# Decoder, layer 3 cross attention: 128 (head, token) rows a unit instead of 100

## The chip, the cores and the metric

One Trainium2 chip, one of its cores. The metric is the device time of one execution in microseconds (us), the median of several runs. The profile is one further execution, taken by the hardware profiler. Engines are written as the profile writes them: PE is TensorE (PEld its weight loads), DVE is VectorE, ACT is ScalarE, POOL is GpSimd, SP is the engine whose queue issues most DMAs.

## The reference, cut to what matters

The program is a four-layer decoder for 16 images of 100 text tokens, width 128, float32. Each layer has self attention, cross attention to 1444 context vectors of width 96 per image, and a feed-forward block. Only the attention part of layer 3's cross attention is changed:

```
Q = (x_text @ Wq).reshape(Bb, Tt, H, DH)          # 16 images, 100 tokens, 4 heads of 32
K = (x_vision @ Wk).reshape(Bb, Gg, H, DH)        # 1444 keys an image
scores = jnp.einsum('bthd,bghd->bhtg', Q, K) / np.sqrt(DH)
scores = jnp.where(vision_mask[:, None, None, :], scores, -jnp.inf)
topv, topi = jax.lax.top_k(scores, K_TOP)         # K_TOP = 32
probs = jax.nn.softmax(topv, axis=-1)
attn = jnp.zeros_like(scores).at[bi, hi, ti, topi].set(probs)
attn_mean = attn.mean(axis=1)                     # over the 4 heads
c_t = jnp.einsum('btg,bgd->btd', attn_mean, x_vision @ Wv)
c_t = c_t * text_mask[..., None]
```

So every one of 16 x 4 x 100 = 6400 score rows of 1444 numbers has its 32 largest found, the softmax is taken over these alone, the four heads are averaged, and the average weighs the context. `c_t` (tile `CT` in the kernel) then steers the rest of the layer: a norm, a long convolution over tokens (`kern`), and a feed-forward block.

## The kernel before, in words

The kernel is written with a tile framework: the author writes tiles and operations, a scheduler orders the instructions of each engine, and semaphores are put in where a tile is written and read, or its buffer is used again. An engine executes its own list strictly in order. A pool with `bufs=n` hands out n buffers in turn; who asks for one more waits until the oldest has been read for the last time.

The whole program runs layer after layer. The changed stage, `l3_xattn`, begins with small weight products (`xattn_weights`), the layer norm of `X` into `XN` (DVE and POOL, L264) and its transpose into `XT` (`turn`). Then it loops over the images `b`:

- `fetch(b)` brings in the context twice: `ct` (channels in partitions, for the scores; its last row is filled by POOL at L1330 from the byte mask `vm`) and `cn` (keys in partitions, for the weighted sum). Both come through SP's queue, one image ahead.
- `queries` folds the key projection into the query: 4 small matmuls on PE (L635), then one DVE add (L637). The result `qk` has 4 heads x 100 tokens as columns.
- `head(b, h, qk)` treats one head: 100 rows. Three matmuls (L1340) put 100 x 1444 scores into one of two PSUM score buffers (`psS`, `bufs=2`, three banks each). DVE then finds the 32 largest of every row in four rounds of `max` (the 8 largest of a row, L1346) and `match_replace` (overwrites those 8 by a mark, L1347), the first round from PSUM and the others in the copy `wk`. ACT computes the exponential of all scores (L1352, bias `nm`, the negated row maximum). One more DVE pass (L1354) keeps the exponential where the mark stands, sets the rest to zero and adds up the row. Small DVE operations give `rs`, one over the sum times 0.25 times the token's mask; ACT multiplies the row by `rs` (L1361, L1363), and POOL adds the heads into `AM` (L1364).
- `mean(b - 1)`, emitted in the middle of image b: 12 transposes of `AM` (L1371), three ACT copies (L1374), 12 matmuls with `cn` (L1377), a copy `cc`, one matmul with the value weights (L1382) and the copy into `CT` (L1383).

Two score buffers and three `cn` buffers let PE run ahead of DVE. After the stage come the norm, the convolution (99 DVE passes, L1431) and the feed-forward blocks.

Of the kernel before, what the change touches and what calls it, by code (L numbers as in the profile page):

```python
# [9 lines left out]
F32 = mybir.dt.float32  # L10
U8 = mybir.dt.uint8
AF = mybir.ActivationFunctionType
ALU = mybir.AluOpType
AX = mybir.AxisListType
PSUM = bass.MemoryType.PSUM

B, S, D = 16, 100, 128
NT = B * S
G4 = 4 * S
NG = B // 4  # L20
CK = 1444
CD = 96
CA = CD + 1
NCH = 12
CKP = NCH * 128
NH = 16
BIG = 1e30
MARK = -3e38
# [13 lines left out]
def _layout(i):  # L42
    f = np.float32
    arr = {}
# [3 lines left out]
    ctx = i["ctx_768"]  # L48
    arr["ctxT"] = np.concatenate([ctx.transpose(0, 2, 1), np.ones((B, 1, CK), f)], axis=1)
    cn = np.zeros((B, CKP, CA), f)  # L50
# [2 lines left out]
    arr["ctxn"] = cn.reshape(B, NCH, 128, CA).transpose(0, 2, 1, 3)  # L53
    arr["x"] = i["x"].transpose(1, 0, 2)
    arr["tmask"] = i["mask_BxS_bf1"].T.copy().view(np.uint8)
    arr["vmask"] = i["mask_BxS2_bf1"].view(np.uint8)

    rows = [
# [31 lines left out]
    p, q = np.arange(128)[:, None], np.arange(128)[None, :]  # L90
# [2 lines left out]
    e = np.arange(16)[:, None, None]  # L93
    sel = np.zeros((128, 8, 128))
    sel[:16] = e == 2 * np.arange(8)[None, :, None] + (np.arange(128) // 64)[None, None, :]
    consts = [
        ("ident", (p == q)), ("hmask", p // 8 == np.arange(NH)[None, :]), ("tri", tri), ("tri3", tri3),
        ("rev", np.broadcast_to(16.0 - np.arange(16), (128, 16))), ("sel", sel.reshape(128, -1)),
    ]
# [50 lines left out]
    for r in range(4):  # L150
        for a in range(4):
            blk, o, h = (0, 9 * a, 3 * r + a) if a < 3 else (1, 0, 12 + r)
            d = slice(8 * h, 8 * h + 8)
# [31 lines left out]
class Decoder:  # L185
# [438 lines left out]
            self.copy(wvo[:, h0 : h0 + m, :].rearrange("p h e -> p (h e)"), ps[:CA, : m * D])  # L624
        return wqk, cq, wvo

    def queries(self, b, nh, wqk, cq, wp, psA):

        nc = self.nc
        qk = wp.tile([CA, nh, S], F32, tag="qk", name="qk")  # L630
        for h0 in range(0, nh, 4):
            m = min(4, nh - h0)
            ps = psA.tile([128, 512], F32, tag="ps", name="ps_qk")
            for j in range(m):
                nc.tensor.matmul(ps[:CA, j * S : (j + 1) * S], lhsT=wqk[:, h0 + j, :],  # L635
                                 rhs=self.XT[:, b * S : (b + 1) * S], start=True, stop=True)
            nc.vector.tensor_tensor(  # L637
                qk[:, h0 : h0 + m, :], ps[:CA, : m * S].rearrange("p (h q) -> p h q", h=m),
                cq[:, h0 : h0 + m].unsqueeze(2).to_broadcast([CA, m, S]), ALU.add,
            )  # L640
        return qk
# [654 lines left out]
    def l3_xattn(self):  # L1296
        nc, tc, ins = self.nc, self.tc, self.ins
        with ExitStack() as outer:
# [6 lines left out]
            with ExitStack() as st:  # L1305
                xw = st.enter_context(tc.tile_pool(name="xw", bufs=1))
                wp = st.enter_context(tc.tile_pool(name="wp", bufs=2))
                cx = st.enter_context(tc.tile_pool(name="cx", bufs=2))
                psS = st.enter_context(tc.tile_pool(name="psS", bufs=2, space=PSUM))
                psA = st.enter_context(tc.tile_pool(name="psA", bufs=2, space=PSUM))  # L1310
                wqk, cq, _ = self.xattn_weights("l3x", 4, 32, 1.0 / math.sqrt(32.0), xw, psA)
                nc.vector.memset(cq[CD:CA, :], 1.0)
                self.ln(xw, self.X, self.XN, 1e-5)
                self.turn(psA, self.XN, self.XT)
                tm4 = xw.tile([S, B], F32, name="tm4")
                nc.vector.tensor_scalar(tm4, self.tm, 0.25, None, ALU.mult)
                AM = []
                for j in range(2):
                    t = xw.tile([S, CKP], F32, name=f"AM{j}")
                    nc.gpsimd.memset(t[:, CK:], 0.0)  # L1320
                    AM.append(t)
                ctx = {}

                def fetch(b):
                    ct = cx.tile([CA, CK], F32, tag="ct", name="ct")
                    nc.sync.dma_start(out=ct[:CD], in_=ins["ctxT"][b, :CD])
                    vm = cx.tile([CA, CK], U8, tag="vm", name="vm")
                    nc.sync.dma_start(out=vm[CD:CA], in_=ins["vmask"][b : b + 1])

                    nc.gpsimd.tensor_scalar(ct[CD:CA], vm[CD:CA], -1.0, BIG, ALU.add, ALU.mult)  # L1330
                    cn = cx.tile([128, NCH, CA], F32, tag="cn", name="cn", bufs=3)
                    nc.sync.dma_start(out=cn, in_=ins["ctxn"][b])
                    ctx[b] = ct, cn

                def head(b, h, qk):
                    ct, am = ctx[b][0], AM[b % 2]
                    ps = psS.tile([128, CKP], F32, tag="s", name="ps_s")
                    for n0 in range(0, CK, 512):
                        n1 = min(n0 + 512, CK)
                        nc.tensor.matmul(ps[:S, n0:n1], lhsT=qk[:, h, :], rhs=ct[:, n0:n1], start=True, stop=True)  # L1340
                    s = ps[:S, :CK]
                    wk = wp.tile([S, CK], F32, tag="wk", name="wk")
                    m8 = wp.tile([S, 4, 8], F32, tag="m8", name="m8")
                    cur = s
                    for j in range(4):
                        nc.vector.max(m8[:, j, :], cur)  # L1346
                        nc.vector.match_replace(wk, m8[:, j, :], cur, MARK)  # L1347
                        cur = wk
                    nm = wp.tile([S, 1], F32, tag="nm", name="nm")
                    nc.vector.tensor_scalar(nm, m8[:, 0, 0:1], -1.0, None, ALU.mult)  # L1350
                    ex = wp.tile([S, CK], F32, tag="ex", name="ex")
                    nc.scalar.activation(ex, s, AF.Exp, bias=nm)  # L1352
                    sm = wp.tile([S, 1], F32, tag="sm", name="sm")
                    nc.vector.scalar_tensor_tensor(ex, wk, MARK, ex, ALU.is_equal, ALU.mult, accum_out=sm)  # L1354

                    nc.vector.scalar_tensor_tensor(sm, m8[:, 0, 0:1], -0.5 * BIG, sm, ALU.is_gt, ALU.mult)
                    rs = wp.tile([S, 1], F32, tag="rs", name="rs")
                    nc.vector.reciprocal(rs, sm)
                    nc.vector.tensor_tensor(rs, rs, tm4[:, b : b + 1], ALU.mult)
                    if h == 0:  # L1360
                        nc.scalar.activation(am[:, :CK], ex, AF.Copy, scale=rs)  # L1361
                    else:
                        nc.scalar.activation(ex, ex, AF.Copy, scale=rs)  # L1363
                        nc.gpsimd.tensor_tensor(am[:, :CK], am[:, :CK], ex, ALU.add)  # L1364

                def mean(b):
                    am, cn = AM[b % 2], ctx[b][1]
                    ps = psS.tile([128, CKP], F32, tag="s", name="ps_am")
                    p3 = ps.rearrange("p (c q) -> p c q", c=NCH)
                    for c in range(NCH):  # L1370
                        nc.tensor.transpose(p3[:, c, :S], am[:, c * 128 : (c + 1) * 128], self.ident[:S, :S])  # L1371
                    pt = wp.tile([128, NCH, S], F32, tag="pt", name="pt", bufs=1)
                    for g in range(3):
                        nc.scalar.copy(pt[:, 4 * g : 4 * g + 4, :], p3[:, 4 * g : 4 * g + 4, :S])  # L1374
                    pc = psA.tile([128, 512], F32, tag="ps", name="ps_c")
                    for c in range(NCH):
                        nc.tensor.matmul(pc[:CD, :S], lhsT=cn[:, c, :CD], rhs=pt[:, c, :],  # L1377
                                         start=(c == 0), stop=(c == NCH - 1))
                    cc = wp.tile([CD, S], F32, tag="cc", name="cc")
                    nc.scalar.copy(cc, pc[:CD, :S])  # L1380
                    pd = psA.tile([128, 512], F32, tag="ps", name="ps_ct")
                    nc.tensor.matmul(pd[:, :S], lhsT=self.l3x_v, rhs=cc, start=True, stop=True)  # L1382
                    nc.scalar.copy(CT[:, b * S : (b + 1) * S], pd[:, :S])  # L1383

                fetch(0)
                for b in range(B):
                    if b + 1 < B:
                        fetch(b + 1)
                    qk = self.queries(b, 4, wqk, cq, wp, psA)
                    for h in range(4):  # L1390
                        head(b, h, qk)
                        if h == 1 and b > 0:
                            mean(b - 1)
                mean(B - 1)

            with ExitStack() as st:
                w1, wp, psG, psM, psO = self.ffn_pools(st)
# [6 lines left out]
                a, _ = self.rat["mg"]  # L1404
# [106 lines left out]
```

## Time and profile before

| what | value |
|---|---|
| time, median of 3 runs | 5873.32 us (5872.37 to 5873.75) |
| the profiled execution's own time | 5845.56 us |
| its span, first to last instruction | 5843.8 us |
| mean granted PE clock over the span | 0.863 of full |
| PE, DVE, ACT, POOL busy share of the span | 82%, 57%, 29%, 16% |
| the changed stage: first `max` to the last of the 256 `match_replace` | 4342.0 to 5323.3 us |
| the stage's set-up before, and the last image's `mean` after it | 4324.5 to 4342.0, 5323.3 to 5341.4 us |

How to read it: the profiled execution ran 28 us below the median of the others, so a sum made from its durations is compared with its own 5845.56 us and then carried over to the median. "Busy" counts instructions that are at work; a wait is not busy. A PE matmul in float32 leaves two records, so 12 matmuls show as `x24`. PEclk is the share of PE's full clock that was granted.

### The profile page before, as it was taken

What the parts mean: (1) busy time and instruction counts of PE and PEld (TensorE: products, weight loads), DVE (VectorE), ACT (ScalarE), POOL (GpSimd) and SP (SyncE); (2) the same over time, 40 slices, a digit from 0 to 9 for tenths busy, and PEclk for the clock granted to TensorE, in tenths of its full rate; (3) what the DMA queues carried; (4) which work ended last, traced back from release to release, by engine and by line L of the source; (5) the groups of instructions that cost most, each with busy time, mean ns of one, the idle gap of its engine ahead of it and who ended that gap; (6) DMA issues with size and microseconds to landing.
All of it is one profiled execution on the core that took longest, in us unless ns stands there. A gap on an engine that the chain in (4) does not pass through costs nothing.

```text
span 5843.8 us, 71087 instructions
## 1 busy us (share of the span) xinstructions
PE 4771.2 (82%) x29792; PEld 3240.0 (55%) x29792; DVE 3306.3 (57%) x5595; ACT 1695.8 (29%) x2620; POOL 933.9 (16%) x609
## 2 busy tenths in 40 slices
PE   6999999999999998899899999998773333333399
PEld 4777777777776766556645555555451211211277
DVE  5444444444444346535455555551569999998643
ACT  2333333333332222314324344343122222221122
POOL 6200000000000036117610000001641111112200
PEclk9899999999999987889879999996675666556599
DMA  1100000000000001200000000000010000000000
GB/s 49 64 17 9 17 9 17 9 17 9 13 1 1 1 2 57 83 1 1 1 21 9 13 9 9 9 5 1 1 67 16 20 20 16 20 12 0 0 2 5
DMA packets 17638, 92.12 MB, mean 16 GB/s; under 512 B 2428, under 2 KB 2909, under 8 KB 16130
## 3 DMA queue, kind: packets, MB, share of 16 engines
q1 hardware_dynamic: 16954, 86.62, 4.9%
q8 instruction: 235, 3.85, 0.3%
q10 hardware_dynamic: 364, 0.96, 0.1%
q14 instruction: 85, 0.70, 0.0%
HBM read 86.74 MB, written 0.82 MB: 15 GB/s over the span
## 4 chain that ended last, share of the span: by engine, by line
PE 68%; DVE 23%; POOL 5%; issue 2%; ACT 1%; DMA 0%; POOLq 0%; ACTq 0%; DVEq 0%
PE ps_t L718 9%; PE ps_s L692 9%; DVE m L1346 7%; DVE wk L1347 6%; PE ps_st L902 6%; PE ps_s L868 5%; PE ps_o L1060 4%; PE ps_pv L333 4%; PE ps_s L704 4%; PE ps_s L298 3%; PE pg L1074 3%; PE pu L1076 3%; PE ps_O L884 3%; DVE y L1431 2%; PE ps_v L830 2%
## 5 line engine op out<-in xcount | busy, mean ns | idle before, releaser
L1340 PE MATMUL ps_s<-ct,qk 97*100 97x512 f32 (+1 forms) x384 | 266.2, 849 | 495.2 <-ACT ex L1352 495.1
L694 DVE TENSOR_REDUCE nm<-ps_s 128x1 f32<-128x1444 f32 (+2 forms) x224 | 372.0, 1661 | 470.8 <-PE ps_s L692 470.7
L870 DVE TENSOR_REDUCE pm<-ps_s 100x2 f32<-100x968 f32 (+1 forms) x384 | 433.6, 1158 | 339.9 <-PE ps_s L868 338.8
L718 PE MATMUL ps_t<-cn,pt 128*128 128x97 f32 (+2 forms) x5376 | 619.6, 271 | 0.9 <-DVE X L735 0.8
L718 PEld LDWEIGHTS ps_t<-cn,pt 128*128 128x128 f32 (+2 forms) x5376 | 599.7, 186 | 10.9 <-issue 6.5
L692 PE MATMUL ps_s<-ct,qk 97*128 97x512 f32 (+5 forms) x1344 | 590.1, 575 | 2.1 <-ACT pt L710 2.1
L710 ACT COPY pt<-ps_s 128x512 f32<-128x512 f32 (+2 forms) x448 | 250.7, 560 | 1030.6 <-PE ps_s L704 1013.6
L904 ACT ACTIVATE pt<-ps_st 121x400 f32<-121x400 f32 (+1 forms) x768 | 348.2, 501 | 470.6 <-PE ps_s L868 242.5
L902 PE MATMUL ps_st<-q,K 32*121 32x300 f32 (+3 forms) x3072 | 464.9, 373 | 7.4 <-ACT pt L904 7.3
L902 PEld LDWEIGHTS ps_st<-q,K 32*121 32x121 f32 (+1 forms) x3072 | 339.5, 186 | 190.7 <-ACT pt L904 107.9
L1340 PEld LDWEIGHTS ps_s<-ct,qk 97*100 97x100 f32 x384 | 87.1, 246 | 640.8 <-ACT ex L1352 524.6
L868 PE MATMUL ps_s<-K,q 32*100 32x484 f32 (+1 forms) x1536 | 402.0, 605 | 0.3 <-DVE pm L870 0.2
L704 PE MATMUL ps_s<-cst_sb,P 128*128 128x128 f32 (+2 forms) x2688 | 360.6, 269 | 13.2 <-ACT P L695 11.3
L704 PEld LDWEIGHTS ps_s<-cst_sb,P 128*128 128x128 f32 (+2 forms) x2688 | 301.8, 142 | 110.3 <-issue 87.0
L692 PEld LDWEIGHTS ps_s<-ct,qk 97*128 97x128 f32 (+2 forms) x1344 | 232.6, 186 | 229.2 <-issue 223.9
L695 ACT ACTIVATE P<-ps_s,nm 128x1444 f32<-128x1444 f32 (+2 forms) x224 | 328.0, 1464 | 98.7 <-DVE nm L694 92.8
L1347 DVE MATCH_REPLACE8 wk<-m,wk 100x1444 f32<-100x1444 f32 x192 | 314.9, 1644 | 0.0
L1346 DVE MAX8 m<-wk 100x8 f32<-100x1444 f32 x192 | 311.6, 1649 | 0.0
L333 PEld LDWEIGHTS ps_pv<-va,pt 100*100 100x100 f32 x2560 | 267.8, 184 | 37.5 <-DVE pt L247 17.4
L333 PE MATMUL ps_pv<-va,pt 100*100 100x9 f32 (+1 forms) x2560 | 267.0, 245 | 13.1 <-DVE pt L247 8.2
L1079 ACT ACTIVATE sl<-pg 128x400 f32<-128x400 f32 x256 | 129.1, 504 | 423.7 <-PE pg L1074 264.4
L1352 ACT ACTIVATE ex<-ps_s,nm 100x1444 f32<-100x1444 f32 x64 | 93.7, 1464 | 541.1 <-DVE nm L1350 533.4
(434 smaller groups left out, 7523.5 us busy)
## 6 DMA issues: line engine op xcount, KB each, us to landing
ct<-in_ctxT SPq DMA_DIRECT2D x64, 541.5 KB
cn<-in_ctxn SPq DMA_DIRECT2D x48, 582.0 KB
l0f_sb<-in_l0f SPq DMA_DIRECT2D x3, 2048.0 KB
l3f_sb<-in_l3f SPq DMA_DIRECT2D x3, 2048.0 KB
wts_sb<-in_wts SPq DMA_DIRECT2D x1, 2576.5 KB
l0x_raw<-in_l0x SPq DMA_DIRECT2D x1, 1800.0 KB
l1f_sb<-in_l1f SPq DMA_DIRECT2D x1, 1728.0 KB
X<-in_x SPq DMA_DIRECT2D x1, 800.0 KB
```

The source lines that it names most:

```text
L333: nc.tensor.matmul(pv[:, h, :], lhsT=pt[:, h, :], rhs=va[:, h, :], start=True, stop=True)
L692: nc.tensor.matmul(ps[:nr, n0:n1], lhsT=q, rhs=ctx[b][0][:, n0:n1], start=True, stop=True)
L694: nc.vector.tensor_reduce(nm[:nr], ps[:nr, :CK], AX.X, ALU.max, negate=True)
L704: nc.tensor.transpose(p3[:, c, :nr], P[u % 2][:nr, c * 128 : (c + 1) * 128], self.ident[:nr, :nr])
L718: nc.tensor.matmul(ps[:nr, :CA], lhsT=pt[:, c, :nr], rhs=cn[:, c, :], start=(c == 0), stop=(c == NCH - 1))
L868: nc.tensor.matmul(ps[:S, j, : n1 - n0], lhsT=q0[r : r + 32, a, :], rhs=K[r : r + 32, a // 3, : n1 - n0], start=True, stop=True)
L870: nc.vector.tensor_reduce(pm[:, a, 2 * half : 2 * half + 2, n], ps[:S, :, : n1 - n0], AX.X, ALU.max)
L902: nc.tensor.matmul(ps[: n1 - n0, cols], lhsT=K[r : r + 32, k, at : at + n1 - n0], rhs=q1[r : r + 32, cols], start=True, stop=True)
L904: nc.scalar.activation(pt[: n1 - n0, r // 32, :], ps[: n1 - n0, :G4], AF.Exp)
L1340: nc.tensor.matmul(ps[:S, n0:n1], lhsT=qk[:, h, :], rhs=ct[:, n0:n1], start=True, stop=True)
L1346: nc.vector.max(m8[:, j, :], cur)
L1347: nc.vector.match_replace(wk, m8[:, j, :], cur, MARK)
```

## The change

- The unit of work becomes 128 score rows. The 400 (head, token) rows of an image are cut into three units of 128 rows, and the last 16 rows of each image go into a shared unit: for a group of 4 images one unit takes 32 columns of each image's `qk` into partitions 32j to 32j+31 (of which the upper 16 rows are new, the lower 16 are weighted zero). 64 units of 100 rows become 48 + 4 = 52 units of 128 rows.
- `nm` moves from DVE to POOL, and the exponential `ex` is emitted right after the first `max`.
- The masking pass leaves DVE. ACT computes the exponential of `wk` (where the 32 marks give zero), and POOL subtracts it from `ex`: what is left are the 32 chosen ones. The row sum comes from a small ACT exponential of the 32 maxima (`e8`, with `accum_out`).
- The scaling by `rs`, the adding of the heads and the transposes become one accumulated matmul: `rw` (128 x 100, made on POOL) holds `rs` times 0.25 times the mask at the column of the row's token, and `gather` multiplies each of the 12 key blocks of `ex` with it into a PSUM tile of three banks that adds up over the image's units.
- The score pool has one buffer instead of two, to make room for that accumulator. `ct` has 5 buffers, `cn` 2, `vm` 1, `qk` 5, and `ex` alternates between `EX0` and `EX1` (`EX2`, `EX3` for the shared units). Four images are fetched ahead. `cn` is now loaded in `keys(b)`, at the image's first unit.
- A new input `tmr` (the masks by row) is loaded at the stage's start, and the constants grow by `tok` (128 x 400).

```diff
-                psS = st.enter_context(tc.tile_pool(name="psS", bufs=2, space=PSUM))
+                psS = st.enter_context(tc.tile_pool(name="psS", bufs=1, space=PSUM))
+                psT = st.enter_context(tc.tile_pool(name="psT", bufs=1, space=PSUM))
...
+                def scores(g, b, u):
+                    ps = psS.tile([128, CKP], F32, tag="s", name="ps_s")
+                    rest = [(j, 4 * g + j) for j in range(4)] if b is None else [(None, b)]
+                    for n0 in range(0, CK, 512):
+                        n1 = min(n0 + 512, CK)
+                        for j, bb in rest:
+                            q = qks[bb].rearrange("p h q -> p (h q)")
+                            if j is None:
+                                o, q = ps[:, n0:n1], q[:, 128 * u : 128 * u + 128]
+                            else:
+                                o, q = ps[32 * j : 32 * j + 32, n0:n1], q[:, 4 * S - 32 :]
+                            nc.tensor.matmul(o, lhsT=q, rhs=ctx[bb][:, n0:n1], start=True, stop=True)
+                    return ps
...
                     for j in range(4):
                         nc.vector.max(m8[:, j, :], cur)
+                        if j == 0:
+                            nc.gpsimd.tensor_scalar(nm, m8[:, 0, 0:1], -1.0, None, ALU.mult)
+                            nc.scalar.activation(ex[:, :CK], s, AF.Exp, bias=nm)
                         nc.vector.match_replace(wk, m8[:, j, :], cur, MARK)
                         cur = wk
-                    nc.vector.tensor_scalar(nm, m8[:, 0, 0:1], -1.0, None, ALU.mult)
-                    nc.scalar.activation(ex, s, AF.Exp, bias=nm)
-                    nc.vector.scalar_tensor_tensor(ex, wk, MARK, ex, ALU.is_equal, ALU.mult, accum_out=sm)
+                    nc.scalar.activation(e8, m8.rearrange("p a b -> p (a b)"), AF.Exp, bias=nm, accum_out=sm)
+                    nc.scalar.activation(wk, wk, AF.Exp, bias=nm)
+                    nc.gpsimd.tensor_tensor(ex[:, :CK], ex[:, :CK], wk, ALU.subtract)
                     nc.vector.scalar_tensor_tensor(sm, m8[:, 0, 0:1], -0.5 * BIG, sm, ALU.is_gt, ALU.mult)
                     nc.vector.reciprocal(rs, sm)
-                    nc.vector.tensor_tensor(rs, rs, tm4[:, b : b + 1], ALU.mult)
-                    if h == 0:
-                        nc.scalar.activation(am[:, :CK], ex, AF.Copy, scale=rs)
-                    else:
-                        nc.scalar.activation(ex, ex, AF.Copy, scale=rs)
-                        nc.gpsimd.tensor_tensor(am[:, :CK], am[:, :CK], ex, ALU.add)
+                    nc.gpsimd.tensor_scalar(rw, sel[:, u, :], rs, tm, ALU.mult, ALU.mult)
...
+                def gather(b, ex, rw, r0, r1, first, last):
+                    if first:
+                        acc[b] = psT.tile([128, 3, 512], F32, tag="m", name="ps_m")
+                    for c in range(NCH):
+                        nc.tensor.matmul(acc[b][:, c // 4, (c % 4) * S : (c % 4 + 1) * S], lhsT=ex[r0:r1, c * 128 : (c + 1) * 128],
+                                         rhs=rw[r0:r1], start=first and c % 4 == 0, stop=last, skip_group_check=True)
...
-                    for c in range(NCH):
-                        nc.tensor.transpose(p3[:, c, :S], am[:, c * 128 : (c + 1) * 128], self.ident[:S, :S])
-                    for g in range(3):
-                        nc.scalar.copy(pt[:, 4 * g : 4 * g + 4, :], p3[:, 4 * g : 4 * g + 4, :S])
+                    nc.scalar.copy(pt.rearrange("p (g c) q -> p g (c q)", g=3), acc.pop(b)[:, :, : 4 * S])
...
+                    ex = EX[2 + g % 2] if b is None else EX[nx % 2]
+                    rw = weigh(ps, ex, tm, u)
...
+                    if i + 1 < len(units):
+                        ps = begin(i + 1)
+                    if pend is not None:
+                        gather(b0, ex0, rw0, 0, 128, u0 == 0, False)
+                        if u0 == NU - 1:
+                            gather(b0, *left[b0 // 4], 32 * j, 32 * j + 32, False, True)
+                            mean(b0, cns.pop(b0))
```

## The prediction

> **What bounds the kernel now.** I first cut the span into stretches and read the busy time of each engine in the changed stage, its set-up and its end.
>
> ```profile
> core 0: us, PE busy (x) PEld busy (x) DVE busy (x) ACT busy (x) POOL busy (x), PEclk, DMA share, GB/s
> 4325.00:4342.00 17.00, 11.59 (x46) 7.54 (x46) 8.51 (x44) 3.07 (x5) 13.12 (x11) 0.57 0.64 207
> 4342.00:5325.00 983.00, 357.46 (x1060) 180.56 (x1058) 980.16 (x1163) 214.36 (x202) 168.09 (x60) 0.60 0.07 21
> 5325.00:5342.00 17.00, 8.04 (x44) 7.01 (x44) 1.34 (x12) 4.65 (x7) 6.45 (x2) 0.57 0.00 1
> ```
>
> DVE is busy for 980 of 983 us: the stage is DVE's list, end to end. PE works 36% of it at a granted clock of 0.60, ACT 22%, POOL 17%. Next, the groups of that stage, to see what the list consists of and what the helpers cost, and two rows of the waits.
>
> ```profile
> L1347 DVE MATCH_REPLACE8 wk<-m,wk 100x1444 f32<-100x1444 f32 x192 | 314.9, 1644 | 0.0
> L1346 DVE MAX8 m<-wk 100x8 f32<-100x1444 f32 x192 | 311.6, 1649 | 0.0
> L1364 POOL TENSOR_TENSOR AM<-AM,ex 100x1444 f32<-100x1444 f32 x48 | 155.0, 3229 | 455.6 <-ACT ex L1363 455.5
> L1354 DVE SCALAR_TENSOR_TENSOR ex<-wk,ex 100x1444 f32<-100x1444 f32 x64 | 105.6, 1651 | 0.0
> L1352 ACT ACTIVATE ex<-ps_s,nm 100x1444 f32<-100x1444 f32 x64 | 93.7, 1464 | 541.1 <-DVE nm L1350 533.4 <-PE ps_s L1340 7.7
> L1359 DVE TENSOR_TENSOR rs<-rs,tm 100x1 f32<-100x1 f32 x64 | 28.4, 444 | 0.3
> L264 POOL TENSOR_SCALAR XN<-X,ln_mv,ln_rs 100x128 f32<-100x128 f32 x8 | 6.5, 828 | 2.2 <-DVE ln_rs L261 2.2
> ```
>
> ```profile
> ACT ex L1352 <- DVE nm L1350: 533.4, 59, 21.3
> DVE m L1346 <- PE ps_s L1340: 3.9, 8, 2.1
> ```
>
> ACT, PE and POOL wait for DVE; DVE hardly for anyone. Last the timeline, for the price of a hand-over from engine to engine, and of the same PE work at two granted clocks:
>
> ```profile
> 4704.14 1.65 DVE L1347 MATCH_REPLACE8 wk<-m,wk 100x1444 f32<-100x1444 f32 x1
> 4704.26 1.47 ACT L1352 ACTIVATE ex<-ps_s,nm 100x1444 f32<-100x1444 f32 x1 [17.91 <-DVE nm L1350]
> 4706.43 1.50 ACT L1363 ACTIVATE ex<-ex,rs 100x1444 f32<-100x1444 f32 x1 [0.70 <-DVE rs L1359]
> 4708.07 3.23 POOL L1364 TENSOR_TENSOR AM<-AM,ex 100x1444 f32<-100x1444 f32 x1 [18.34 <-ACT ex L1363]
> 4718.60 3.92 PE L1377 MATMUL ps_c<-pt,cn 128*96 128x100 f32 x24 [0.58 <-ACT pt L1374]
> 4740.77 5.13 PE L1340 MATMUL ps_s<-ct,qk 97*100 97x512 f32 x6 [14.93 <-ACT ex L1352]
> ```
>
> ```profile
> 509.33 2.82 PE L718 MATMUL ps_t<-cn,pt 128*128 128x97 f32 x24
> 3306.49 0.88 PE L884 MATMUL ps_O<-pt,V 121*32 121x300 f32 x16
> ```
>
> `nm` ends at 4704.14 and ACT starts at 4704.26: 0.12 us. ACT ends at 4707.93 and POOL starts at 4708.07: 0.14 us. A run of 24 records (12 matmuls of some 100 columns) takes 3.92 us here and 2.82 us in layer 0, where PE is always busy.
>
> **The change part by part.**
>
> *DVE's own work.* From the first max to the last replace 64 heads take 981.3 us. The mask pass leaves (105.6 us), so do `nm` (64 x about 0.07 = 4.2) and L1359 (28.4; its mean of 444 ns holds a wait for scores). What is left is 843.1; 9 us are the 16 query adds, which stay. (843.1 - 9) / 64 = 13.03 us a unit. A pass over 128 rows is priced like one over 100, since L694's passes over 128 x 1444 last 1.66 us as well. 52 units: 52 x 13.03 + 9 = 687 us. If DVE still never waited, the stage would lose 294 us.
>
> *The new loop.* It will wait. The built order of DVE's list, with M0 to M3 the max passes and R0 to R3 the replaces, dot unit, repeats this pattern:
>
> ```
> R3.19 s.19 M1.20 r.19 R1.20 M2.20 M0.21 R2.20 R0.21 M3.20 M1.21 R3.20 s.20 R1.21 r.20 M0.22
> ```
>
> Between R3 of unit i and R0 of unit i+2 there are always five long passes and two or three short ones: 5 x 1.6 + 0.3 = 8.3 us. And R0 of i+2 waits for the exponential of i+2: both read the score tile, and the listing has the replace wait for ACT. (The Trainium skill, "PSUM — Partial Sum Buffer", section "PSUM bank collisions raise a hardware error", says two engines must not read one bank at once; no run here shows that collision.) That exponential writes `EX[i % 2]`, so it waits for the gather of unit i, which waits for POOL. From the end of R3 of i: hand-over 0.12, exponential of `wk` 1.48 (L1352, L1363), hand-over 0.14, subtraction 3.23 (L1364), `rw` 0.65 (L264's 0.83 for 128 columns and two pointers, times 100/128), hand-over 0.1, gather 3.9, last matmul and hand-over 0.2, exponential 1.46, hand-over 0.1: 11.4 us. POOL's mask row of `ct` (L1330, 1.39 us once an image) and ACT's copies of `mean` get in between now and then: 0.5 more on average, 11.9. DVE stands 11.9 - 8.3 = 3.6 us a unit, 48 x 3.6 = 173 us. The intervals of different units do not overlap on DVE's list, so these add up.
>
> Two prices in it need a choice. The gather: 3.9 (L1377, this stage) or 2.8 (L718, same weights 128*128)? The Trainium skill, "TensorE: Matmul & The Clock Gate", Part 1, says PE falls to half clock after about 3.4 us of idleness and is released only by as long a busy time. PE will idle some 5 us before each gather, while ACT and POOL work, and the stage's 0.60 shows how such gaps end; I take 3.9. With 2.8 the stall is 2.5 and the sum 53 us lower. The subtraction: L1364 has the same form, beside the same DVE passes; L314, POOL's two-input pass of 1600 columns, takes 2.86 us, so 2.58 for 1444 is the low end (31 us less). 3.23 is the nearer row.
>
> A rule of the Trainium skill speaks against this part: "GPSIMD Engine Reference", section "Performance versus the Vector engine", has the vector engine about twice as fast on elementwise work. The rows agree on the size (3.23 against 1.65) but not on what follows: POOL was idle for 83% of the stage, so by busy time the move is free. By the loop it is not. With the mask left on DVE the units would cost 52 x 1.65 = 86 us more, but the chain would lose exponential, subtraction and two hand-overs (5.0 us) and fit into the slack: 687 + 86 = 773, plus the 21 below. By my sum the moved mask costs more than it saves; against the kernel before, the smaller number of units still wins.
>
> *Image ends.* Every third unit adds on PE: 12 gather matmuls with the shared unit, the copy of the accumulator, 12 matmuls with `cn`, and only then the scores of unit i+3, which has no second score buffer. From R3 of i: 6.2 to the gather, 3.9, 2.8 to 3.9, copy 1.5, 2.8 to 3.9, scores 2.6 to 5.1 (5.13 is L1340 at half clock, half of it at full), 0.3: 20.1 to 24.8. DVE has ten long passes, short ones and one stall before its max of i+3: about 20.0. Cost 0.1 to 4.8; PE has by then been busy for a while, so I take 1.3: 16 x 1.3 = 21 us.
>
> *Shared units.* 12 matmuls of 512 columns in four 32-column strips. L884 has that shape: 16 records in 0.88 us, where 8 of 300 and 8 of 100 columns one after the other need 8 x 0.25 + 8 x 0.083 = 2.7 us at the full clock (from L1340's slow 0.855 us for 512 columns, by length and halved). Three run at once, so 6.8 us slow, 20.5 if they don't. Where one starts, R0 directly follows M0, or the four query adds come late: some 5.5 us for each of 4. Against that, two intervals at each of the three inner boundaries have a shared unit between them and no stall: 6 x 3.6 = 22. I book zero.
>
> *Set-up and end.* The first scores now need four `ct`. The DMAs carry 207 GB/s in the row above, about 2.7 MB up to the fourth `ct`: done by 4336. The mask rows are later: `vm` has one buffer, so each byte row waits for POOL to have used the last, and POOL has the norm (6.5 us) and L280 (3.8 us) between. In POOL's order the fourth follows at about 4346.3; with 6.8 us of scores the first max starts at 4353 instead of 4342: +11. `tmr` (128 small rows) lands under the norm. `tok` is 205 KB in a load that is not awaited before 28 us: nothing. At the end exponential, subtraction, `rw`, two gathers, copy, `cn`: 18 us, as before.
>
> *Off the path.* ACT loses 64 scalings and gains 52 x (1.46 + 0.25); POOL loses 48 additions and gains 52 subtractions, `rw` and `nm`, 230 us in 880; both stay under 30%. `cn` and `ct` stay the same number of bytes, four images ahead; SP holds `ct` behind `cn`, which waits for an old `mean`, still units early.
>
> *Sum.* 687 + 173 + 21 = 881 against 981.3: -100; set-up +11; -89. On the profiled execution 5845.6 - 89 = 5757; the median lies 27.8 us higher: 5784 us.
>
> **The rivals.**
>
> *The loop does not bind.* Gather 2.8, subtraction 2.58, `rw` 0.4: chain 9.4, stall 1.1: 48 x 1.1 = 53 instead of 173, so 5664 us. For it: PE gets 576 matmuls on top of 656 and may stay fast. Against: L1364 lies between 3222 and 3237 ns in all 48 cases.
>
> *PE stays slow and serial.* Image ends at their 4.8 (+56) and shared scores at 20.5 (+14 in the set-up, up to 5 x 3 later): 5784 + 85 = 5869 at worst, 5845 with half of it. Against: L884.
>
> *Slower: POOL sets the pace.* One mechanism at one place: the subtraction on 128 rows. Each us more in it is 48 us more in the stage. At 5.1 us the gain is gone, above 5.4 the kernel is slower; at 6.0 it is 5784 + 133 = 5917. For it: in this stage POOL needs 2.24 ns a column, against 1.79 in L314, so it does feel its neighbours. Against: 3229 ns beside exactly these DVE passes.
>
> **How the numbers follow.** Forecast 0.72, non-binding loop 0.11, slow PE 0.10, POOL's pace 0.07. A measurement of this kernel tells about 0.2%, 12 us, from no change; below 5861.6 counts as faster: all of the first two and most of the third, 0.90; same 0.04, from the ends of the third and fourth; slower 0.06. The range: fast gather and `rw` of 0.4 give 5784 - 53 - 12 = 5719, and halfway from there to the non-binding loop, 5690, is the low end; 5845, half of the slow-PE case, is the high end. Beyond are half of each of these two (0.11) and POOL's pace (0.07).
>
> **What would show it.** Right: DVE busy about 690 us between first max and last replace, 880 apart; R0 (`match_replace` from `ps_s`) waiting for ACT `ex` some 3.6 us each; ACT `ex` waiting for PE `ps_m`; the subtraction at 3.2 us, a gather near 3.9, PEclk 0.6 to 0.7. Wrong: DVE above 90% busy in the stage (the loop does not bind), R0's wait released by POOL's `nm`, or max waiting longest, for PE scores.

## The result, and the profile after

| | before | after |
|---|---|---|
| median of 4 runs | 5873.5 us (5872.4 to 5884.6) | 5818.5 us (5804.2 to 5821.9) |
| ratio to before | | 0.9897, 95% interval 0.9877 to 0.9918 |
| the profiled execution | 5845.6 us | 5817.8 us |
| set-up: 4324.5 to the first max; 4362.4 after | 17.5 us | 24.2 us |
| first max to last replace | 981.3 us | 910.9 us |
| the end, to the last `CT` copy | 18.1 us | 21.0 us |

The kernel became 55 us (1.0%) faster; 5784 was forecast, in a range from 5690 to 5845. In the two traces set-up, stage and end together went from 1016.9 to 956.1 us: 61 less, where the forecast had 89. The profiled executions differ by 28 only; the end of the experiments looks at why.

First the windows of the kernel after, set-up, stage and end (columns: window, length, busy time of PE, PEld, DVE, ACT and POOL, granted PE clock, DMA share, GB/s):

```profile
4362.40:4386.60 24.20, 16.90 (x80) 10.08 (x80) 10.55 (x53) 4.35 (x6) 16.27 (x17) 0.65 0.75 212
4386.60:5297.50 910.90, 569.80 (x2325) 408.89 (x2326) 693.59 (x739) 194.80 (x252) 212.59 (x166) 0.65 0.07 22
5297.50:5318.50 21.00, 17.00 (x89) 15.60 (x88) 4.98 (x39) 3.29 (x5) 3.65 (x2) 0.59 0.00 0
```

DVE was busy for 980 of 983 us before. Now it is busy for 693.6 of 910.9 and stands still for 217: the stage is no longer one engine's list. The waits of that stretch say at whose hands (engine and line waiting, engine waited for, total us, times, longest):

```profile
DVE wk L1383 <- ACT EX L1382: 151.6, 51, 7.0
DVE m L1379 <- PE ps_s L1368: 64.1, 20, 8.0
ACT EX L1382 <- POOL nm L1381: 85.4, 12, 14.1
ACT EX L1382 <- PE ps_m L1404: 326.2, 40, 10.8
PE ps_m L1404 <- POOL rw L1396: 159.4, 42, 13.5
```

The rows of `EX` and `ps_m` make one chain: a unit's first replace waits for the exponential (L1382), that for the gather (L1404), that for POOL's `rw`. So it is in 40 of the 52 units, and 131 of the 152 us lie there. In the other 12, each shared unit and the two behind it, POOL's `nm` is the last thing that the exponential waits for, and the replace stands for 20 us in all. The second row is the max waiting for scores; 5.0 of its 64.1 us lie ahead of the first max, so 59 are inside. One turn of the chain in the timeline, from the last replace of a unit to the first replace of the unit after next:

```profile
4717.42 1.65 DVE L1383 MATCH_REPLACE8 wk<-m,wk 128x1444 f32<-128x1444 f32 x1
4719.16 1.50 ACT L1389 ACTIVATE wk<-wk,nm 128x1444 f32<-128x1444 f32 x1 [2.77 <-DVE sm L1392]
4720.74 3.23 POOL L1390 TENSOR_TENSOR EX<-EX,wk 128x1444 f32<-128x1444 f32 x1 [10.96 <-ACT wk L1389]
4723.96 0.43 POOL L1396 TENSOR_SCALAR rw<-cst_sb,rs,tmr 128x100 f32<-128x100 f32 x1
4724.44 5.45 PE L1404 MATMUL ps_m<-rw,EX 128*128 128x100 f32 x24 [4.84 <-POOL rw L1396]
4729.98 1.46 ACT L1382 ACTIVATE EX<-ps_s,nm 128x1444 f32<-128x1444 f32 x1 [9.32 <-PE ps_m L1404]
4731.48 0.09 DVE L1383 MATCH_VALUE_LOAD wk<-m,ps_s 128x8 f32 x1 [4.05 <-ACT EX L1382]
```

From 4719.07 to 4731.56 the chain takes 12.5 us; DVE has five long passes beside it, 8.4 us, and stands for 4.05. The long passes that DVE has between these two replaces are called the cover from here on. The gather's duration decides how long DVE stands: of the 29 gathers that ran alone and in one piece, 9 took 2.8 to 2.9 us at a granted clock of 1.00, 13 took 5.4 at 0.50, and 7 between 4.1 and 4.9, at 0.57 to 0.68. After a gather of 2.92 the replace waits 1.5 to 1.9 us, after one of 5.44 mostly 4.0 or 4.1: the difference is that of the gathers.

### The profile page after: what moved, and what is told of

Same layout as the page of the kernel before. It is cut to its first block, busy times and chain, and to the rows that moved or that the text cites. A ratio compares the mean times of both kernels' runs of the same rounds, so it can differ in the third digit from the quotient of the medians.

```text
span 5815.6 us, 73656 instructions
## 1 busy us (share of the span) xinstructions
PE 5033.4 (87%) x31136; PEld 3497.5 (60%) x31136; DVE 3022.3 (52%) x5172; ACT 1675.8 (29%) x2668; POOL 978.4 (17%) x719
## 5 line engine op out<-in xcount | busy, mean ns | idle before, releaser
L912 PE MATMUL ps_st<-q,K 32*121 32x300 f32 (+3 forms) x3072 | 478.2, 383 | 7.4 <-ACT pt L914 7.3
L878 PE MATMUL ps_s<-K,q 32*100 32x484 f32 (+1 forms) x1536 | 421.5, 632 | 0.3 <-DVE pm L880 0.2
L1404 PE MATMUL ps_m<-rw,EX 128*128 128x100 f32 (+1 forms) x1536 | 274.8, 357 | 162.2 <-POOL rw L1396 159.4
L1404 PEld LDWEIGHTS ps_m<-rw,EX 128*128 128x128 f32 (+1 forms) x1536 | 261.8, 266 | 214.3 <-POOL rw L1396 199.8
L1368 PE MATMUL ps_s<-ct,qk 97*128 97x512 f32 (+3 forms) x384 | 240.6, 851 | 148.0 <-DVE wk L1383 146.3
L1390 POOL TENSOR_TENSOR EX<-EX,wk 128x1444 f32<-128x1444 f32 x52 | 168.1, 3233 | 542.0 <-ACT wk L1389 537.8
L1383 DVE MATCH_REPLACE8 wk<-m,wk 128x1444 f32<-128x1444 f32 x156 | 256.9, 1647 | 0.0
```

Of the source, the lines that this page charges most:

```text
L878: nc.tensor.matmul(ps[:S, j, : n1 - n0], lhsT=q0[r : r + 32, a, :], rhs=K[r : r + 32, a // 3, : n1 - n0], start=True, stop=True)
L912: nc.tensor.matmul(ps[: n1 - n0, cols], lhsT=K[r : r + 32, k, at : at + n1 - n0], rhs=q1[r : r + 32, cols], start=True, stop=True)
L1404: nc.tensor.matmul(acc[b][:, c // 4, (c % 4) * S : (c % 4 + 1) * S], lhsT=ex[r0:r1, c * 128 : (c + 1) * 128], rhs=rw[r0:r1], start=first a ...
```

## The experiments

Three theories. *The loop*: two `EX` buffers tie the exponential of unit i+2 to the gather of unit i, and that chain is longer than the passes beside it. *The score buffer*: PE's cold matmuls and the single score tile bind, and the replace's wait is their other face. *POOL's pace*: every us of the subtraction is a us of every unit. Stage and waits are always taken from the first max to the last replace in the profile, so the wait ahead of the first max, 5.0 to 10.8 us, is not among them as it is in the rows of the views. DVE was busy for 687 to 705 us of the stage, except where the mask is on DVE (774 and 785).

| run | stage | replace waits | max waits | program, median | ratio to before |
|---|---|---|---|---|---|
| after | 911 | 152 | 59 | 5818 | 0.990 (0.988 to 0.992) |
| e1_ex3 | 847 | 77 | 82 | 5732 | 0.976 (0.970 to 0.983) |
| e2_mask_dve | 865 | 54 | 30 | 5748 | 0.978 (0.972 to 0.985) |
| e3_mean_late | 937 | 175 | 64 | 5826 | 0.995 (0.992 to 0.998) |
| e4_sub_half | 914 | 162 | 58 | 5806 | 0.989 (0.981 to 0.997) |
| p1_order | 736 | 4 | 11 | 5615 | 0.959 (0.957 to 0.961) |
| p2_sub_half_pinned | 881 | 104 | 76 | 5756 | 0.984 (0.982 to 0.987) |
| p3_mask_dve_order | 803 | 4 | 0 | 5684 | 0.972 (0.969 to 0.974) |
| p4_warm_pinned | 912 | 144 | 45 | 5804 | 0.994 (0.991 to 0.996) |
| p5_order_late | 736 | 4 | 11 | 5626 | 0.960 (0.958 to 0.961) |
| p6_order_twice | 862 | 4 | 29 | 5749 | 0.980 (0.978 to 0.982) |
| p7_six | 909 | 129 | 44 | 5789 | 0.988 (0.987 to 0.990) |
| p8_ex3_pinned | 820 | 25 | 70 | 5711 | 0.972 (0.969 to 0.975) |

### Four edits with the scheduler free (e1 to e4)

```diff
# e1_ex3 (and one buffer for cn, cc and the shared rw)
-                    ex = EX[2 + g % 2] if b is None else EX[nx % 2]
+                    ex = EX[3 + g % 2] if b is None else EX[nx % 3]
# e2_mask_dve, in place of e8, the exponential of wk and the subtraction
+                    nc.vector.scalar_tensor_tensor(ex[:, :CK], wk, MARK, ex[:, :CK], ALU.is_equal, ALU.mult, accum_out=sm)
# e3_mean_late: the copy pt stays; cn matmuls, cc, ct follow the next unit's scores
# e4_sub_half
-                    nc.gpsimd.tensor_tensor(ex[:, :CK], ex[:, :CK], wk, ALU.subtract)
+                    nc.gpsimd.tensor_tensor(ex[:, : CK // 2], ex[:, : CK // 2], wk[:, : CK // 2], ALU.subtract)
```

> A third EX buffer for the own units, so that the exponential of unit i waits for the gather of unit i-3 and not i-2 (to make room, `cn`, `cc` and the shared `rw` get one buffer). The stage from first max to last replace lasts 910.9 us in the changed kernel: DVE busy 694, the first replace waits 152 for ACT, the max waits 64 for scores. Theory 1 (the two EX buffers close a loop over ACT, POOL, PE that binds): the replace's wait falls from 152 to under 20; at the 16 image ends the scores lose the time that the stall gave them, so the max's wait grows from 4 to about 7 us each, 64 to about 115; stage about 825, gain 85. Theory 2 (the single score tile binds and the replace's wait is only its other face): the whole wait moves to the max, stage within 20 of 911. Theory 3 (POOL's pace binds): POOL needs 3.9 us of 17 a unit, so no third outcome is expected of it: no change either.

Measured: stage 847, the replace's wait halved, the max's 82. The gain of 64 is most of the 85 forecast, but 77 us of wait at the replace was not forecast.

> 128-row units, one-matmul gather and everything else as in the changed kernel, but the mask stays one DVE pass (`scalar_tensor_tensor` with the sum), so no e8, no exponential of wk, no subtraction on POOL. Theory 1 (prediction): DVE busy 694 + 52 x 1.65 = 780; the chain from the last replace to the next exponential loses 5.0 us and gets a pass more of slack, so the replace's wait falls from 152 to under 30; the max's wait stays or falls (64 to 20): stage 790 to 850, that is 60 to 120 shorter than with the mask on ACT and POOL. Theory 2 (PE's scores and gathers bind): stage stays near 911 with the waits at the max. Theory of the change itself (DVE's list is the price): stage 86 longer, about 995.

Measured: stage 865, 46 shorter than with the mask moved, just outside the range; DVE busy 774, against 780 computed. But the scheduler also drew up a new list for DVE: six or seven max and replace passes of cover in 46 of its 50 intervals. So the 46 us belong to the mask pass and the scheduler's order for it together; the comparison with the order held is p3 against p1.

> Only the order on PE is changed: the 12 matmuls with `cn` and the final projection of an image are issued after the next unit's scores, not before them; the copy of the accumulator stays where it is. Theory 1: the max's wait at image ends (64) falls to about 15, the replace's wait (152) stays within 25 of it: stage about 865. If the max's wait is not the image end but the cold scores of every unit, the stage stays within 15 of 911. If the loop takes over what the max no longer waits, the replace's wait grows by what the max's falls, and the stage stays too.

Measured: stage 937, 26 longer. The max waits no less (64), and the replace longer (175, up to 9.2 us at a time). The expectation failed; since the scheduler had also moved DVE's passes a little, this run alone does not say why, and that stays open.

> POOL subtracts only the first 722 of 1444 columns, so keys of the second half keep their full exponential: 1.6 us less in one place of the loop. Theory 1 (every us of the chain is a us of stall): 1.6 x 48 = 77 off the replace's wait, 152 to about 75, and some us off the image ends too: stage 815 to 835. Theory 2 (PE's order or the score tile binds): under 25 off. The subtraction itself would show 1.6 us if POOL's price goes by columns, more if there is a fixed part.

Measured: no gain at all, 914, although the subtraction did halve:

```profile
L1390 POOL TENSOR_TENSOR EX<-EX,wk 128x722 f32<-128x722 f32 x51 | 87.1, 1708 | 541.4 <-issue 244.1 <-ACT wk L1389 228.7 <-PE ps_s L1368 67.7
```

Taken at its word this refutes the loop. But the timeline of this run shows four long passes, not five, between a last replace and the first replace of the unit after next, and the listing of DVE's built order says the same: four in 37 of 50 intervals, where the changed kernel has five in 38, three or four in 5 and six or seven in 7. With the subtraction shorter, the scheduler had drawn the replace one pass forward. The chain lost 1.5 us and the cover 1.65. In e1 it took two passes away (three in 32 intervals). So the order of DVE's list had to be held.

### The order itself, and the order held (p1, p2, p3, p8)

`tc.add_manual_dep` puts an instruction behind another on its engine without a wait. With it the list of all max and replace passes was tied: in p2, p4 and p8 to exactly the order of the changed kernel, in p1, p3, p5 and p6 to this one:

```diff
+                order = [dv[0]["M0"]]
+                for i, d in enumerate(dv):
+                    order += [d[k] for k in ("R0", "M1", "R1", "M2", "R2")]
+                    order += [dv[i + 1]["M0"]] if i + 1 < len(dv) else []
+                    order += [d[k] for k in ("M3", "R3", "K") if k in d]
+                for p, q in zip(order, order[1:]):
+                    tc.add_manual_dep(q.ins, p.ins.name, mybir.DependencyInfo(mybir.DependencyClass.NoSync, mybir.DependencyReason.DATA), reason="order")
```

> Only the order of DVE's list is changed, by ordering edges without a wait: unit i's passes run as R0 M1 R1 M2 R2, the first max of unit i+1, M3 R3. Between the last replace of unit i and the first replace of unit i+2 there are then always eight long passes instead of five. No instruction, buffer or duration changes. Theory 1 (the chain exponential, subtraction, rw, gather, exponential of 12.6 us in the timeline stands against the passes the list happens to put beside it): eight passes are 8 x 1.65 + 0.6 = 13.8 us, more than 12.6, so the replace's wait falls from 152 to under 20. Image ends: the max of unit i+3 comes after 13 passes, 22 us, its scores after 21 to 24: 0 to 2 each, up to 32 for 16. Stage from first max to last replace 695 to 745 instead of 911, program about 5635. Theory 2 (PE's clock and score tile bind, the replace's wait is their other face): the wait moves to the max, stage above 860. Theory 3 (POOL sets the pace): POOL waits now as well; stage above 860.

Measured, windows and DVE's waits of the stage:

```profile
4370.77:5106.35 735.58, 477.47 (x2334) 337.16 (x2334) 702.72 (x739) 191.47 (x252) 214.32 (x166) 0.77 0.08 27
DVE m L1383 <- PE ps_s L1368: 15.6, 4, 5.1
DVE sm L1396 <- ACT e L1391: 11.4, 15, 1.2
DVE wk L1387 <- ACT EX L1386: 4.1, 1, 4.1
```

The replace waits once, in the first unit. 175 us of the stage are gone with the same instructions and buffers, and the program takes 5614.6 us, 0.959 (0.957 to 0.961) of the kernel before. POOL is busy for 214 us as ever. PE's clock rose with it from 0.65 to 0.77, and 28 of the 29 gathers that ran alone took 2.8 to 3.3 us. The timeline shows what changed ahead of them:

```profile
4699.89 5.07 PE L1368 MATMUL ps_s<-ct,qk 97*128 97x512 f32 x6 [5.86 <-DVE rs L1398]
4704.80 5.67 PE L1408 MATMUL ps_m<-rw,EX 128*128 128x100 f32 x48
```

The scores (slow, after 5.86 us of idleness) now run while POOL subtracts, and the gather follows them without a gap, at 0.118 us a record; in the five-pass turn above PE stood 4.84 us before the gather, and it took 0.227. So the order changed two things at once, the cover and the gather's duration. No run here changes the one cleanly without the other, and how the 175 us divide between them stays open.

> Again only the first 722 columns are subtracted (keys of the second half keep their full exponential), but DVE's list is tied to exactly the order of the changed kernel, with five passes in the slack; in the earlier run the scheduler had used the shorter modelled time to put four there. Theory 1: 1.52 us less (3.23 to 1.71) in 40 to 48 units: the replace's wait falls from 152 to 80 to 90, the max's wait at image ends falls from 64 to about 45; stage 820 to 840. If the stage stays above 895, the subtraction is not on the path, and theory 1 is wrong in this link.

Measured: stage 881, 30 less, where 70 to 90 was expected. The replace's wait fell by 48, not by 62 to 72; the max's rose by 17 instead of falling. The subtraction is on the path, but a us of it is worth 20 us of stage, not 48: part of what the replace no longer waits the max waits for scores, and 14 of the 17 us are at the three units that follow a shared one.

> Three EX buffers for the own units again (one buffer each for `cn`, `cc` and the shared `rw`), but now DVE's list is tied to exactly the order of the changed kernel; in the earlier run with three buffers the scheduler had also changed the order (three passes of cover instead of five, stage 847). Theory 1: the exponential of unit i+2 no longer waits for the gather of unit i, so the replace's wait falls from 152 to under 30; the max's wait at image ends grows from 64 to 100 to 130, because the scores there still come behind gather, copy and `cn` matmuls; stage 815 to 850. If the replace still waits over 100, the buffer is not what holds the exponential. If the stage is below 770, the image ends were only an echo of the stall.

Measured, DVE's waits:

```profile
DVE m L1383 <- PE ps_s L1368: 79.2, 17, 9.2
DVE sm L1396 <- ACT e L1391: 30.7, 9, 6.1
DVE wk L1387 <- ACT EX L1386: 25.2, 30, 2.3
ACT EX L1386 <- POOL nm L1385: 268.4, 52, 16.7
```

With the order held and one buffer more, the replace's wait falls from 152 to 25 and the stage to 820, and what the exponential waits for last is now `nm` in all 52 units, the gather in none. That is the loop, shown by its one link. Of the 126 us that the replace no longer waits, 91 reach the stage; the max waits for scores for 70, 11 more than before though less than the 100 to 130 expected, and `sm` waits for the small exponential for 31 instead of 4.

> The mask back as one DVE pass after R3, on 128-row units, with DVE's list in the order of eight passes. Theory 1: nothing waits any more, DVE's own work is the price: 694 + 52 x 1.65 = 780, plus 0 to 20: stage 780 to 800. Against the same order with the mask on ACT and POOL it is then 60 to 85 slower, so that the move of the mask pays where the order gives it room, and not where it doesn't (earlier run: 865 with the mask on DVE, 911 with it moved). If PE's scores bind, stage above 830 with the max waiting.

Measured: 803, 3 above the range, with DVE busy for 785. In the eight-pass order the moved mask is worth 67 us (803 against 736); with the scheduler free to order each of the two it costs 46 (865 against 911).

### The clock, the pace of POOL, and how many passes are enough (p4, p5, p6, p7)

```diff
# p4_warm_pinned, ahead of each gather of an own unit
+                        for _ in range(10):
+                            nc.tensor.matmul(pw[:, : 4 * S], lhsT=self.ident, rhs=sel.rearrange("p u q -> p (u q)"), start=True, stop=True)
# p6_order_twice, after the subtraction
+                    nc.gpsimd.tensor_tensor(ex[:, :CK], ex[:, :CK], wk, ALU.subtract)
# p7_six: the order is R0 M1 R1 M2, next M0, R2 M3, next R0, R3
# p5_order_late: p1 and the edit of e3
```

> Order as in the changed kernel, and 10 extra matmuls of 400 columns on PE between a unit's scores and the gather (their result is not used), about 3.3 us at the full clock and 6.7 at half. Does PE's idle time before the gather cost the clock? In the changed kernel 9 of 29 whole gathers took 2.9 us, 17 took 5.4. Theory A: with the gap filled nearly all gathers take 2.9 and scores 2.6 instead of 5.1, granted clock above 0.9, the replace's wait falls from 152 to 50 to 70 and the max's from 64 to 15: stage 780 to 830. Theory B (the clock does not come back): the extra matmuls at half speed are themselves in front of the gather and add up to 3 us a unit: stage above 950.

Measured: neither. The clock rose to 0.86 and most gathers of 24 records took 2.8 or 2.9 us, but the stage stayed at 912. (Of the 29 gathers in the changed kernel 13 took 5.4 us, not 17; 7 lie in between.) The extra matmuls stand in the way: eleven of these gathers started 1.3 to 7.5 us after their `rw` was ready, because the extra matmuls had not ended. Here `rw` was ready at 4751.42:

```profile
4745.97 6.88 PE L1458 MATMUL ps_w<-cst_sb 128*128 128x400 f32 x20
4752.69 2.82 PE L1408 MATMUL ps_m<-rw,EX 128*128 128x100 f32 x24
```

So this run does not price the clock. The comparison inside the kernel after does (1.5 to 1.9 us of stall behind a gather of 2.92, 4.04 behind one of 5.44), and in p1 the fast gathers come without extra work.

> DVE's list in the order of eight passes, and besides the matmuls with `cn` issued after the next unit's scores. With eight passes alone the stage lasts 736 us, DVE busy 703, and only 16 us are waited for scores, all at the four shared units, 11 for the small exponential e8. Theory 1: the image ends no longer bind, so the late mean brings nothing: stage 725 to 740, program within 15 of the order of eight passes (5614). If image ends still cost, 10 to 20 shorter.

Measured: 736, the same as p1; 5625.6 us (5610.9 to 5630.1) against 5614.6 (5603.1 to 5630.3). With this order the late matmuls gain nothing: the max waits only at shared units (three times 3.5 us), and besides only `sm` waits, 0.4 to 1.2 us at a time.

> POOL subtracts twice in every unit (keys outside the 32 get a negative weight), in the order of eight passes: POOL's work per unit doubles, 3.24 us more in the chain, some 52 x 3.24 = 168 us more POOL work. In the order of eight passes the exponential starts 0.5 to 1.8 us after the gather's end and ends about 2 us before the replace that waits for it, so 2.5 to 3.8 us of room are left. Theory 1 (chain against passes): at most 0.7 us a unit come through: stage 736 to 775. POOL's pace theory (each us of subtraction is 48 us of stage): stage about 890. The forecast's slower rival stands on the second.

Measured: between the two theories, 862. POOL was busy for 378 us. The replace still does not wait; the wait comes out elsewhere:

```profile
DVE sm L1397 <- ACT e L1391: 117.2, 31, 7.1
4705.01 10.81 PE L1409 MATMUL ps_m<-rw,EX 128*128 128x100 f32 x48 [1.25 <-POOL EX L1395]
4710.55 1.46 ACT L1386 ACTIVATE EX<-ps_s,nm 128x1444 f32<-128x1444 f32 x1 [12.53 <-PE ps_m L1409]
4717.36 0.16 DVE L1397 SCALAR_TENSOR_TENSOR sm<-m,sm 128x1 f32<-128x1 f32 x1 [7.08 <-ACT e L1391]
```

`e8` stands behind the exponential in ACT's list, that waits for the gather, and `sm` of the unit before stands ahead of the replace in DVE's list. The forecast for the loop left out that a later gather is a slower one too: with a pause ahead of it again, 11 of the 29 gathers that ran alone took 5.4 us and 6 more over 4. 3.24 more for the subtraction and 2.6 for the gather, less 2.5 to 3.8 of room, are 2.0 to 3.3 a unit where the gather is slow, at most 105 to 175 for 52 units; 127 were measured. This account was made after the run.

> The same kernel with six long passes between the last replace of unit i and the first replace of unit i+2 in every unit: R0 M1 R1 M2, the first max of unit i+1, R2 M3, the first replace of unit i+1, R3. Six passes are 10.3 us of cover, against a chain of 12.6 with a gather of 5.44 and 10.1 with one of 2.92. Theory 1: a stall of 0 to 2.3 a unit, and the max of unit i+3 comes two passes earlier than with eight, 0 to 4 at each image end: stage 770 to 850, between 736 (eight) and 911 (mostly five). If it is 736 to 750 the number of passes is not what matters but only that M0 and R0 stand apart; if above 900, something other than the chain.

Measured: no better than the scheduler's order, 909. Behind many gathers of 5.44 the forecast holds: the replace waits 2.4 us instead of 4.04, one pass less. But no gather that ran alone took less than 4.3 us, after six image ends the replace waits 7.3 us, and `sm` and the query add wait for 36 us where they waited for 4. By the expectation's own sign (above 900) more than the length of the chain is at work. With six passes each of these gathers still comes after a pause of at least 1.6 us; with eight none but the last of the stage does. The two orders also differ in where the first max stands, so what makes the step from 909 to 736 is not isolated.

### The 33 us that the profiled executions hide

Of the 61 us gained in set-up, stage and end the profiled executions show 28: in the profile of after the stage's set-up starts 38 us later than before, and what follows the stage is 5 us shorter. 27 of these us arise in layer 2's cross attention, which the change does not touch, the other 11 ahead of it. The same 100 us of that layer, before and then after:

```profile
3350.00:3450.00 100.00, 99.95 (x846) 57.08 (x839) 52.54 (x62) 40.70 (x89) 0.00 (x0) 1.00 0.05 12
3350.00:3450.00 100.00, 99.95 (x774) 57.99 (x773) 50.65 (x61) 35.56 (x78) 0.00 (x0) 0.91 0.05 12
```

PE is busy all the time in both, but was granted half the clock for some 17 us in the second. The time from the first to the last record of that stage's output matmuls (`ps_O`, L884 before and L894 after) was 1020.6 us in before's profile and 1048.0 in after's; in p2 and p7, which have all of the change, it was 1020.6 and 1020.5, in p1 1042.4, in e3 1099.8. So these 27 us belong to the execution, not to the change. Where a program's time moves by tens of us, the stage's own time in the trace is the safer measure.

## Why the prediction was right, and where not

- **DVE's own work: right.** 687 forecast, 693.6 measured.
- **The loop: right in mechanism, somewhat too large.** With the 22 us that the forecast took off beside shared units, it was put at 151; the stall behind gathers was 131. Its 3.6 a unit stand against 4.04 behind a gather of 5.44, 3.2 behind one of 4.55 and 1.5 to 1.9 behind one of 2.92. p8 removes it by a buffer alone; p1 removes it by the order, with the faster gathers that come along. Of the terms, the subtraction was 3.23 as priced, `rw` 0.42 instead of 0.65, and the gather's 3.9 stands for two states that both occur; the 29 alone averaged 4.4. The five passes of cover that "always" lie there were five in 38 of 50 intervals.
- **Image ends and shared units: the mis-sized terms.** "PE has by then been busy for a while, so I take 1.3": 21 us forecast, and some 38 measured, where the max mostly waited 1.4 to 3.7 us. Shared units were put at 22 us of late starts and measured 41: 21 lie in three waits of the max of 6 to 8 us, as PE's list has a gather between the strips of scores, and 20 in replaces that wait for the exponential behind `nm`. PE had not been kept fast: the 48 records of both gathers took 7.4 to 10.8 us against 6.7 to 7.8 in the working. The Trainium skill, "TensorE: Matmul & The Clock Gate", Part 1, has the full clock come back after about 3.4 us of sustained work. In the kernel after that is so in part: six gathers of 48 records were granted it 3.6 to 4.6 us after their start, but two had a granted clock of 0.50 through all of their 10.81 us. Where they differ, the measurement decides.
- **Set-up and end:** +11 forecast and +6.7 measured; 18 and 21.
- **Together:** stage 911 against 881. The 30 missing are image ends (+17), shared units (+19), the loop (-20), DVE's own work (+7) and, with smaller waits, about 7 us more. That the loop and the shared units missed by as much in opposite directions is luck.
- **"The moved mask costs more than it saves": right in sign, the size off.** 794 was worked out for the mask on DVE, 865 measured (waits for the replace and the scores were left, 54 and 30), in an order of the scheduler's own. With the order of eight passes held for both it turns round (803 against 736). The rule of the Trainium skill's "GPSIMD Engine Reference", "Performance versus the Vector engine", prices the pass rightly (3.23 against 1.65 us), but by p1 and p3 it does not decide: with that order POOL's dearer pass is the better one.
- **What the prediction lacked:** it took the order of DVE's list as given, and subtracted five passes from the chain. Changing that order gained 175 us, more than any other edit here.
- **Rivals.** A loop that does not bind was put at 5664 us; that is reached, and passed, only with the order changed (p1 and p5). Its sum left out the 0.5 us that the loop's own sum adds for POOL's and ACT's other work; with it the rival stands at 5688. In the same way half of the slow-PE case is 5827, not the 5845 taken as the high end. The measured 5818 lies inside either way. Slow PE was half true, at image ends. POOL's pace, 48 us for each us of subtraction, was not met: 20 in p2, where it becomes shorter, and, in the order of eight passes, 39 in p6, where it becomes longer and the gather with it.

## What to carry to other kernels

When work moves from the bound engine to helpers, count the passes that the bound engine's list really has between the giving and the taking back, in the built order, and compare them with the chain's length; a scheduler can give a shortened chain back as less cover, as it did in e4. An experiment that changes a duration must hold that order, or it measures the scheduler too. Before adding a buffer (91 us here) or moving an operation back (46, with the scheduler free), try moving the waiting instruction down its own list (175).

## What the runs showed of the hardware

- A run of 12 float32 matmuls with 128*128 weights and 100 columns took 2.82 us at a granted clock of 1.00 and 5.44 at 0.50. The pause ahead of it does not decide alone: in the kernel after, 2.8 to 2.9 us came behind pauses of 0 to 2.5 us, 5.44 behind pauses of 1.7 us and more. All 232 changes of the granted clock in that trace lie whole multiples of 3.41 us apart, so it also matters where a run falls on that grid.
- Six score records that themselves ran slow for 5.0 to 5.15 us were followed at once by a gather at or near the fast pace in p1 (2.8 to 3.3 us).
- `MAX8` and `MATCH_REPLACE8` over 1444 columns took 1.65 to 1.66 us with 128 partitions, as with 100 before.
- POOL's subtraction took 1.71 us for 722 columns and 3.23 for 1444: 2.1 ns a column and about 0.2 us fixed.
